# Two transformer layers on one Trainium2 core: longer bank holds in a planned TensorE order, zero products ahead of the first block, nine-step roots, moments by piece

## The chip, the cores and the metric

The kernel runs on one core of a Trainium2 chip. Its engines are TensorE (PE; its weight loads are PEld), VectorE (DVE), ScalarE (ACT), GpSimd (POOL) and SyncE (SP, which here only issues DMAs). The metric is the device time of one execution in microseconds; the median of three runs is given, and one further execution was profiled.

## The reference

4096 tokens (4 sequences of 1024) of width 256 go through two layers, each an attention-like part and a feed-forward part, with a layer norm after each residual sum:

```python
x = L0_attn_x
x = _layernorm(x + _L0_attn_ref(x, W_xproj, dt_bias, A_log, D))     # state-space (SSD), 2 heads, state 64
x = _layernorm(x + _L0_ffn_ref(x, w1, b1, w2, b2))                  # gelu, hidden 1024
x = _layernorm(x + _L1_attn_ref(x, Wqkv, bqkv, Wout, bout, omega, quad_nodes, quad_weights))
x = _layernorm(x + _L1_ffn_ref(x, router_w, expert_bias, w1, w3, w2, sw1, sw3, sw2))
```

`_L0_attn_ref` projects x to a step size and two state vectors, forms decays from their cumulated sums and adds a within-sequence and a carried part. `_L1_attn_ref` is linear attention with 16 heads of width 16: q and k are normalised (a root), projected by omega, and passed through exp (clipped to 20); running sums of k times v and of k are kept, and the result goes through Wout. `_L1_ffn_ref` has two shared experts and eight routed ones of hidden size 512, two per token, all in float32.

## The kernel before, in words

The tokens are cut into 8 blocks of 512, each a tile x0 to x7 of 128 partitions x 4 x 256. Nearly all matrix products are float32; the trace shows a product of 512 columns as two passes.

*Start.* Lines L121 to L138 issue the loads on SP, in the order wx, xt of block 0, vec0, the other even blocks' xt and x, w1, w2, and so on. The first products (`ssd_block`, `project`, L288) need wx_sb and xt of block 0.

*First part, planned.* The work of the first layer, of the second layer's attention and of most of the shared experts is written as small tasks: `ssd_block` for block i; `ffn_block` (turn_x, hidden, outputs); `attn_front` for each half-block hb (turn_x turns the tokens into xTa, project makes q and k, values makes v, turn_qk turns q and k into qkT, features makes qf and kf); `attn_back` (scores, turn_keys, outputs, advance, turn_state, turn, turn_back, project); `attn_tail` (turn_x into xTr, logits, router); then jobs of the shared experts. TensorE executes them in the order in which `trace_tasks` (L248) emits them; the other engines follow a scheduler.

A Task has a cost, a rank, predecessors with a wait for each, and, if it writes PSUM, a pool, a number of banks and a hold. PSUM has 6 banks in pool 0 (SSD, attention, some shared work) and 2 in pool 1 (feed-forward, other shared work). The planner keeps for each pool the times at which its banks come free in its own reckoning, takes at each step the task that can start first (then the lowest rank), and books the task's banks until its end plus hold:

```python
for k in range(task.banks):
    start = max(start, free[task.pool][k] - task.cost * k / task.banks)
...
task.end = now = start + task.cost
for _ in range(task.banks):
    free[task.pool].pop(0)
    free[task.pool].append(now + task.hold)
```

The hold is a plan, no wait: on the chip a bank's next product waits, by semaphore, until the bank has really been copied out. The default hold is 1.5 (L243). The tasks that the change touches are at L466 (turn_x of ffn_block), L583 to L588 (turn_x, project and turn_qk of attn_front), L728 (turn_keys), L737 (turn_back) and L769 (turn_x of attn_tail).

*Dispatch and routed stage.* When the last router product (ps_r) is done, `dispatch` counts on VectorE and GpSimd which token goes to which expert slot, `invert` turns that into lists by products (ps_id), and meanwhile the shared jobs of six blocks run. Then 69 slots of 128 tokens are gathered, put through their expert and added to acc by indirect DMA (`slot_tiles`), in PSUM banks opened anew.

*Tail.* The shared experts of the last two blocks come in pieces (eight of hidden work and four of output, one per tile, for each block; the loop counts them as n, and the block's last four are outputs), between which the eight last layer norms are placed (`last_norm`, L1071), with PE, DVE and ACT in the written order. `sums` takes moments (BATCH_NORM_STATS2 and its aggregate, L1082 and L1083), `scales` the root, `finish` the scaling on ScalarE and the output DMA. For the last block, the first three tiles are normalised after piece 22, the fourth after the last piece.

`rsqrt` (L183) is called by every layer norm and by the q and k normalisation: a guess by an integer shift, then three Newton rounds of three VectorE instructions (L190 to L192).

Of the kernel before, what the change touches and what calls it, by code (L numbers as in the profile page):

```python
# [23 lines left out]
F32 = mybir.dt.float32  # L24
# [52 lines left out]
def two_layers(ctx: ExitStack, tc: tile.TileContext, x, xT, vecs, cols, wx, w1, w2, wqkv, wout, om, rw, moe, out):  # L77
# [19 lines left out]
    def bank(name, n):  # L97

        return psum[n].tile([P, 512], F32, tag="bank", name=name)
# [20 lines left out]
    rw_sb = const.tile([P, KC, VW], F32, name="rw_sb")  # L120
    nc.sync.dma_start(out=wx_sb, in_=wx)  # L121
    nc.sync.dma_start(out=xts[0], in_=xT[0])
    nc.sync.dma_start(out=vec0, in_=vecs[:NVEC0].partition_broadcast(P))
# [59 lines left out]
    def rsqrt(v, shape, tag):  # L183

        r = sm.tile(shape, F32, tag=f"{tag}_r", name=f"{tag}_r")
        s = sm.tile(shape, F32, tag=f"{tag}_s", name=f"{tag}_s")
        nc.vector.tensor_single_scalar(s.bitcast(I32), v.bitcast(I32), 1, ALU.logical_shift_right)  # L187
        nc.vector.tensor_scalar(r.bitcast(I32), s.bitcast(I32), -1.0, float(0x5F3759DF), ALU.mult, ALU.add)  # L188
        for _ in range(3):
            nc.vector.scalar_tensor_tensor(s, r, -0.5, r, ALU.mult, ALU.mult)  # L190
            nc.vector.tensor_mul(s, s, v)  # L191
            nc.vector.scalar_tensor_tensor(r, s, 1.5, r, ALU.add, ALU.mult)  # L192
        return r
# [235 lines left out]
    def ffn_block(i, before, wk):  # L429
# [35 lines left out]
        r = 10.0 + i  # L465
        last = Task(turn_x, 0.9, r, [(ssd_end[i], 10.0), (before, 0.0)], 1, 2)  # L466
        wait = 4.0
# [19 lines left out]
    def attn_front(hb, wk):  # L487
# [94 lines left out]
        used = used_end.get(hb - 2)  # L582
        t_x = Task(turn_x, 0.45, r, [(qk_end.get(hb - 2), 0.0), (ffn_end[i], 10.0), (constants, 0.0), (attention, 0.0)], 0, 1)  # L583
        t_q = Task(lambda: project(0), 1.8, r, [(t_x, 3.5)], 0, 1)
        t_q = Task(lambda: project(1), 1.8, r, [(t_q, 0.0)], 0, 1)
        t_v = Task(values, 1.8, r + 0.1, [(t_x, 3.0), (used, 0.0)], 0, 1)
        t_k = Task(lambda: turn_qk(1), 0.45, r + 0.2, [(t_q, 12.0), (feat_end.get(hb - 1), 0.0)], 0, 1)
        t_q = qk_end[hb] = Task(lambda: turn_qk(0), 0.45, r + 0.2, [(t_k, 0.0)], 0, 1)  # L588
        t_k = Task(lambda: features(1), 0.95, r + 0.3, [(t_k, 5.0), (used, 0.0)], 0, 4, 4.5)
        feat_end[hb] = Task(lambda: features(0), 0.95, r + 0.3, [(t_q, 5.0), (t_k, 0.0), (t_v, 0.0)], 0, 4, 4.5)  # L590

    def attn_back(hb, wk):
# [128 lines left out]
        for j in range(NJ):  # L721
            n = NJ * hb + j
            r = 5.07 + 0.1 * hb + 0.04 * j
            before = at_tile.get(n - 1, {})
            far = at_tile.get(n - 2, {})
            last = hb % 4 == 3 and j == NJ - 1
            t_c = Task(lambda j=j: scores(j), 1.8, r, [(feat_end[hb], 7.0), (before.get("o"), 0.0)], 0, 4, 2.5)
            t_k = Task(lambda j=j: turn_keys(j), 0.9, r + 0.01, [(feat_end[hb], 6.0), (before.get("s"), 0.0)], 0, 2, 2.0)  # L728
            t_o = Task(
                lambda j=j: outputs(j), 1.6, r + 0.02, [(t_c, 3.0), (before.get("kv"), 1.0), (far.get("to"), 0.0)], 0, 2, 1.4  # L730
            )
            at_tile[n] = dict(o=t_o)
            if not last:
                t_s = at_tile[n]["s"] = Task(lambda j=j: advance(j), 0.5, r + 0.03, [(t_k, 2.5), (before.get("kv"), 0.0)], 0, 1)
                at_tile[n]["kv"] = Task(lambda j=j: turn_state(j), 0.25, r - 0.1, [(t_s, 2.0), (t_o, 0.0)], 0, 1)
            t_t = at_tile[n]["to"] = Task(lambda j=j: turn(j), 0.45, r + 0.04, [(t_o, 1.5), (far.get("oT"), 0.0)], 0, 1, 2.5)
            t_t = at_tile[n]["oT"] = Task(lambda j=j: turn_back(j), 0.25, r, [(t_t, 2.0), (far.get("w"), 0.0)], 0, 1)  # L737
            t_w = at_tile[n]["w"] = Task(lambda j=j: project(j), 0.9, r, [(t_t, 2.5)], 0, 1)
        used_end[hb], proj_end[hb] = t_o, t_w

    def attn_tail(i, wk):
# [26 lines left out]
        r = 5.3 + 0.2 * i  # L768
        t_x = turn_end[i] = Task(turn_x, 0.9, r, [(proj_end[2 * i + 1], 10.0), (tail_end.get(i - 1), 0.0)], 0, 2)  # L769
        t_x = Task(logits, 0.5, r, [(t_x, 5.0)], 0, 1)  # L770
# [299 lines left out]

    def last_norm(i, tiles):  # L1071

# [4 lines left out]
        r = None  # L1077

        def sums():
            st = sm.tile([P, NT, 6], F32, tag="ln_st", name=f"ln_st{i}_{tiles[0]}")  # L1080
            for k, j in enumerate(tiles):
                nc.vector.bn_stats(st[:, k, :], xs[i][:, j, :])  # L1082
                nc.vector.bn_aggr(mv[:, k, :], st[:, k, :])  # L1083

# [6 lines left out]
        def finish():  # L1091
# [7 lines left out]
            )  # L1099

        return sums, scales, finish


# [40 lines left out]
    early, amid, late = [0, 1, 2], [3, 4, 5], [6, 7]  # L1144
    with tc.manual_schedule(engines={mybir.EngineType.PE}):
        for i in range(NBLK):
            ssd_block(i, wk0)
# [97 lines left out]
    with tc.manual_schedule(  # L1245
# [8 lines left out]
        for _, kind, *_, piece in jobs:  # L1254
# [9 lines left out]
            if n in norm:  # L1264
                parts.extend(last_norm(*norm[n]))
                if len(parts) == 3:
                    parts.pop(0)()
            if n == 22:
                ends = last_norm(NBLK - 1, whole[:-1])
                ends[0]()  # L1270
                ends[1]()
# [74 lines left out]
```

## Time and profile before

| | |
|---|---|
| three runs | 1566.04, 1570.9 and 1563.34 us; median 1566.04 |
| profiled execution | 1570.37 us, of which its span is 1568.6 us |
| mean granted TensorE clock over the span | 0.983 |
| DVE, ACT, POOL busy | 761.8, 599.2, 420.3 us |
| moved by DMA | 73.55 MB, mean 47 GB/s; busy share near full in the first slice only |
| largest TensorE groups | routed hidden (L1013) 248.5, shared hidden (L941) 225.9, routed output (L1035) 130.7, feed-forward hidden (L441) 123.5 us |

The profile is a record of one execution. A row of a group names line, engine, operation and tiles (written <- read), count, busy time and the mean of one in ns, and the idle time of the engine ahead of it with what ended it. A row of waits reads: who waited <- for whom: us in total, times, longest. A row of a window has its limits and length, then the busy time (and count) of PE, PEld, DVE, ACT and POOL, the granted TensorE clock, the DMA share and GB/s. A row of the timeline has start and length in us, engine and line. Buffer numbers are left out of names: qkT stands for the qkT of every half-block. What the profile calls the granted clock is the share of its full rate that TensorE was given; before the first record it is shown as 1.00.

### The profile page before, as it was taken

Reading aid. Unit: us, or ns where it says so; the run is one execution under the profiler, and the core shown is the slowest. Engines: PE = TensorE matmul, PEld = TensorE weight load, DVE = VectorE, ACT = ScalarE, POOL = GpSimd, SP = SyncE. Lnnn points to the kernel's source line nnn. Section 1 sums busy time; section 2 is a strip of 40 time slices with the busy share of each in tenths; the row PEclk is TensorE's granted clock in tenths of the full one; section 3 lists DMA queues with packets and bytes.
Section 4 is the critical chain, followed back from the end, with each engine's and each line's share of the span. In section 5 each row is a group of like instructions: output and inputs, shape, how many; then the busy total and the mean of one; then the engine's idle time right before and its main releaser. Section 6 shows DMA issues by size and latency. Waiting matters only on the chain. (4 is left out here: it accounts for less than half of the span.)

```text
span 1568.6 us, 25398 instructions
## 1 busy us (share of the span) xinstructions
PE 1493.9 (95%) x9700; PEld 970.0 (62%) x9700; DVE 761.8 (49%) x2411; ACT 599.2 (38%) x1056; POOL 420.3 (27%) x456
## 2 busy tenths in 40 slices
PE   8999989999999989989999999999999999999997
PEld 5566647575857665755765765556666666666554
DVE  5977735665656475575455456122222222222264
ACT  3463373436364625446547411111222222222132
POOL 5623302322122121221110004012444444443100
PEclk9999999999999999999999999999999999999999
DMA  9000000000000000030101043041223223232431
GB/s 328 1 1 1 1 1 2 27 2 1 28 1 15 15 1 28 2 122 1 48 8 55 15 166 136 24 151 41 46 47 46 46 45 47 45 47 35 91 104 54
DMA packets 49654, 73.55 MB, mean 47 GB/s; under 512 B 8416, under 2 KB 42208, under 8 KB 48000
## 3 DMA queue, kind: packets, MB, share of 16 engines
q1 hardware_dynamic: 35856, 52.19, 9.4%
q0 software_dynamic: 13248, 18.17, 7.5%
q8 instruction: 80, 1.31, 0.4%
q10 hardware_dynamic: 432, 1.57, 0.3%
q14 instruction: 38, 0.31, 0.1%
HBM read 45.93 MB, written 25.99 MB: 46 GB/s over the span
## 5 line engine op out<-in xcount | busy, mean ns | idle before, releaser
L1013 PE MATMUL ps_ge<-w,xeT 128*128 x552 | 248.5, 593 | 1.0 <-issue 1.0
L941 PE MATMUL ps_g<-xTs,w 128*128 128x512 f32 x512 | 225.9, 594 | 5.4 <-ACT sl L949 2.6
L941 PEld LDWEIGHTS ps_g<-xTs,w 128*128 128x128 f32 x512 | 95.6, 190 | 119.3 <-issue 106.1
L1013 PEld LDWEIGHTS ps_ge<-w,xeT 128*128 128x128 f32 x552 | 99.5, 190 | 100.6 <-issue 100.6
L1044 POOL DMA_INDIRECT acc<-ye,back x69 | 109.4, 1585 | 110.1 <-DVE xew L1000 75.6
L1023 DVE TENSOR_TENSOR ge<-se,ps_ge 128x512 f32<-128x512 f32 x69 | 47.5, 688 | 178.7 <-PE ps_ge L1013 175.8
L441 PE MATMUL ps_h<-xT,w_sb 128*128 128x512 f32 x256 | 123.5, 627 | 9.1 <-ACT hT L444 5.4
L1035 PE MATMUL ps_ye<-w2e,geT 128*128 x552 | 130.7, 380 | 0.9 <-DVE geT L1030 0.9
L988 POOL DMA_INDIRECT xe<-xt,sent x69 | 68.2, 989 | 228.7 <-PE ps_xe L996 166.3
L453 PE MATMUL ps_f<-w_sb,hT 128*128 128x256 f32 x512 | 117.5, 384 | 0.0
L959 PE MATMUL ps_e<-w,gT 128*128 128x256 f32 x512 | 114.6, 380 | 2.1 <-DVE x L968 2.1
L621 POOL TENSOR_TENSOR sc<-sc,mask_le 128x512 f32<-128x512 f32 x32 | 40.9, 1278 | 275.3 <-ACT sc L620 275.3
L959 PEld LDWEIGHTS ps_e<-w,gT 128*128 128x128 f32 x512 | 96.1, 190 | 18.9 <-DVE x L968 3.7
L1035 PEld LDWEIGHTS ps_ye<-w2e,geT 128*128 128x128 f32 x552 | 99.6, 190 | 12.2 <-ACT ye L1043 1.1
L453 PEld LDWEIGHTS ps_f<-w_sb,hT 128*128 128x128 f32 x512 | 96.8, 192 | 15.9 <-issue 3.4
L950 DVE TENSOR_TENSOR gT<-sl,ps_g 128x512 f32<-128x512 f32 x64 | 43.9, 686 | 115.0 <-PE ps_g L941 92.4
L949 ACT ACTIVATE sl<-ps_g 128x512 f32<-128x512 f32 x64 | 38.0, 596 | 156.7 <-PE ps_g L941 143.4
L441 PEld LDWEIGHTS ps_h<-xT,w_sb 128*128 128x128 f32 x256 | 49.7, 201 | 65.5 <-issue 54.8
L1021 ACT ACTIVATE se<-ps_ge 128x512 f32<-128x512 f32 x69 | 41.3, 599 | 121.5 <-PE ps_ge L1013 121.5
L623 DVE TENSOR_TENSOR sc<-ps_sc,mask_le 128x512 f32<-128x512 f32 x96 | 62.7, 685 | 37.5 <-PE ps_sc L611 30.4
L611 PE MATMUL ps_sc<-qf,kf 64*128 64x128 f32 x1024 | 68.0, 281 | 0.6 <-ACT kf L577 0.5
L1000 DVE TENSOR_TENSOR xew<-xe,nth 128x1 f32<-128x1 f32 x69 | 11.0, 160 | 118.2 <-ACT ye L1043 109.9
(257 smaller groups left out, 2485.5 us busy)
## 6 DMA issues: line engine op xcount, KB each, us to landing
w<-in_moe SPq DMA_DIRECT2D x8, 1024.0 KB, 9.1
xt<-in_xT SPq DMA_DIRECT2D x8, 512.0 KB, 9.6
x<-in_x SPq DMA_DIRECT2D x8, 512.0 KB, 10.8
xt<-x SPq DMA_DIRECT2D x8, 512.0 KB, 3.7
td<-xTr SPq DMA_DIRECT2D x16, 256.0 KB, 2.5
w2e<-in_moe SPq DMA_DIRECT2D x8, 512.0 KB, 7.6
x<-acc SPq DMA_DIRECT2D x8, 512.0 KB, 8.4
out<-x SPq DMA_DIRECT2D x7, 512.0 KB, 2.9
```

The source lines that it names most:

```text
L441: nc.tensor.matmul(ps, w1_sb[:, k, m * P : (m + 1) * P], v.xT[:, k, :], start=(k == 0), stop=(k == KC - 1))
L453: nc.tensor.matmul(v.ps[:, j % 2, :], v.hT[:, m, j * P : (j + 1) * P], w2_sb[:, m, :], start=(m == 0), stop=(m == HID0 // P - 1),)
L611: nc.tensor.matmul(ps[s][:, r * P : (r + 1) * P], kf[rows, r, q, tok], qf[rows, r, q, tok], start=True, stop=True)
L623: nc.vector.tensor_mul(t_s, ps_s, mask)
L941: nc.tensor.matmul(ps[s], w[e][:, 2 * s + k, m * P : (m + 1) * P], xT[i][:, k, :], start=(k == 0), stop=(k == KC - 1),)
L950: nc.vector.tensor_mul(gT[i, e][:, m, :], sl, ps[1])
L959: nc.tensor.matmul(ps, gT[i, e][:, m, j * P : (j + 1) * P], w2e[:, m, :], start=(e == 0 and m == 0), stop=(e == NSH - 1 and m == HID // P ...
L988: nc.gpsimd.indirect_dma_start(out=xe, out_offset=None, in_=xt, in_offset=bass.IndirectOffsetOnAxis(ap=sent[:, s : s + 1], axis=0),)
L1013: nc.tensor.matmul(pg[a], xeT[s][:, k, :], w13[:, bass.ds(e * (4 * HID) + (2 * a + k) * HID, HID)], start=(k == 0), stop=(k == KC - 1),)
L1023: nc.vector.tensor_mul(ge[s], se, pg[1])
L1035: nc.tensor.matmul(ps[:, :D], geT[s][:, m, :], w2[:, bass.ds(of[s] * (2 * HID) + m * D, D)], start=(m == 0), stop=(m == HID // P - 1),)
L1044: nc.gpsimd.indirect_dma_start(out=acc, out_offset=bass.IndirectOffsetOnAxis(ap=back[:, s : s + 1], axis=0), in_=ye, in_offset=None, compu ...
```

## The change

Seven edits. (1) The first loads are split: wx and the first xt each in two halves, one half of wx issued by ScalarE. (2) A tile `idle` is filled with zeros by VectorE, and two products of it with itself, written to a bank that nobody reads, stand ahead of the first real products on TensorE. (3) `rsqrt` has nine instructions instead of eleven: the shift and its correction, a round of third order in four, a Newton round in three, with constants folded. (4) For the last block's first three tiles the moments are taken after pieces 20, 21 and 22, one tile each, instead of all three after piece 22. (5) The tasks turn_x (ffn_block, attn_front, attn_tail) hold their banks 4.0, 3.5 and 4.5 instead of 1.5. (6) project and turn_qk of attn_front hold 2.5 and 4.5 instead of 1.5. (7) turn_keys holds 3.0 instead of 2.0 and turn_back 2.5 instead of 1.5. Holds alter only the planner's reckoning, and so the order in which tasks are emitted; the products themselves stay as they are.

```diff
--- before.py
+++ after.py
@@ -118,8 +118,9 @@
     vec = const.tile([P, NVEC - NVEC0], F32, name="vec")
     col = const.tile([P, NCOL], F32, name="col")
     rw_sb = const.tile([P, KC, VW], F32, name="rw_sb")
-    nc.sync.dma_start(out=wx_sb, in_=wx)
-    nc.sync.dma_start(out=xts[0], in_=xT[0])
+    for n in range(2):
+        (nc.scalar, nc.sync)[n].dma_start(out=wx_sb[:, :, n, :], in_=wx[:, :, n, :])
+        nc.sync.dma_start(out=xts[0][:, n, :], in_=xT[0][:, n, :])
     nc.sync.dma_start(out=vec0, in_=vecs[:NVEC0].partition_broadcast(P))
     for i in range(2, NBLK, 2):
         nc.sync.dma_start(out=xts[i], in_=xT[i])
@@ -182,14 +183,18 @@
 
     def rsqrt(v, shape, tag):
 
+
         r = sm.tile(shape, F32, tag=f"{tag}_r", name=f"{tag}_r")
         s = sm.tile(shape, F32, tag=f"{tag}_s", name=f"{tag}_s")
         nc.vector.tensor_single_scalar(s.bitcast(I32), v.bitcast(I32), 1, ALU.logical_shift_right)
         nc.vector.tensor_scalar(r.bitcast(I32), s.bitcast(I32), -1.0, float(0x5F3759DF), ALU.mult, ALU.add)
-        for _ in range(3):
-            nc.vector.scalar_tensor_tensor(s, r, -0.5, r, ALU.mult, ALU.mult)
-            nc.vector.tensor_mul(s, s, v)
-            nc.vector.scalar_tensor_tensor(r, s, 1.5, r, ALU.add, ALU.mult)
+        nc.vector.tensor_mul(s, r, r)
+        nc.vector.tensor_mul(s, s, v)
+        nc.vector.scalar_tensor_tensor(s, s, -10.0 / 3.0, s, ALU.add, ALU.mult)
+        nc.vector.scalar_tensor_tensor(r, s, 5.0, r, ALU.add, ALU.mult)
+        nc.vector.scalar_tensor_tensor(s, r, -0.5 * 0.375**3, r, ALU.mult, ALU.mult)
+        nc.vector.tensor_mul(s, s, v)
+        nc.vector.scalar_tensor_tensor(r, s, 1.5 * 0.375, r, ALU.add, ALU.mult)
         return r
 
     def transposed(t, i, tiles, n, engines):
@@ -463,7 +468,7 @@
                 layernorm(i)
 
         r = 10.0 + i
-        last = Task(turn_x, 0.9, r, [(ssd_end[i], 10.0), (before, 0.0)], 1, 2)
+        last = Task(turn_x, 0.9, r, [(ssd_end[i], 10.0), (before, 0.0)], 1, 2, 4.0)
         wait = 4.0
         for n in range(4):
             last = Task(lambda n=n: hidden(range(2 * n, 2 * n + 2)), 3.5, r + 0.1 * n, [(last, wait)], 1, 2, 2.2)
@@ -580,12 +585,12 @@
 
         r = 5.0 + 0.1 * hb
         used = used_end.get(hb - 2)
-        t_x = Task(turn_x, 0.45, r, [(qk_end.get(hb - 2), 0.0), (ffn_end[i], 10.0), (constants, 0.0), (attention, 0.0)], 0, 1)
-        t_q = Task(lambda: project(0), 1.8, r, [(t_x, 3.5)], 0, 1)
-        t_q = Task(lambda: project(1), 1.8, r, [(t_q, 0.0)], 0, 1)
+        t_x = Task(turn_x, 0.45, r, [(qk_end.get(hb - 2), 0.0), (ffn_end[i], 10.0), (constants, 0.0), (attention, 0.0)], 0, 1, 3.5)
+        t_q = Task(lambda: project(0), 1.8, r, [(t_x, 3.5)], 0, 1, 2.5)
+        t_q = Task(lambda: project(1), 1.8, r, [(t_q, 0.0)], 0, 1, 2.5)
         t_v = Task(values, 1.8, r + 0.1, [(t_x, 3.0), (used, 0.0)], 0, 1)
-        t_k = Task(lambda: turn_qk(1), 0.45, r + 0.2, [(t_q, 12.0), (feat_end.get(hb - 1), 0.0)], 0, 1)
-        t_q = qk_end[hb] = Task(lambda: turn_qk(0), 0.45, r + 0.2, [(t_k, 0.0)], 0, 1)
+        t_k = Task(lambda: turn_qk(1), 0.45, r + 0.2, [(t_q, 12.0), (feat_end.get(hb - 1), 0.0)], 0, 1, 4.5)
+        t_q = qk_end[hb] = Task(lambda: turn_qk(0), 0.45, r + 0.2, [(t_k, 0.0)], 0, 1, 4.5)
         t_k = Task(lambda: features(1), 0.95, r + 0.3, [(t_k, 5.0), (used, 0.0)], 0, 4, 4.5)
         feat_end[hb] = Task(lambda: features(0), 0.95, r + 0.3, [(t_q, 5.0), (t_k, 0.0), (t_v, 0.0)], 0, 4, 4.5)
 
@@ -725,7 +730,7 @@
             far = at_tile.get(n - 2, {})
             last = hb % 4 == 3 and j == NJ - 1
             t_c = Task(lambda j=j: scores(j), 1.8, r, [(feat_end[hb], 7.0), (before.get("o"), 0.0)], 0, 4, 2.5)
-            t_k = Task(lambda j=j: turn_keys(j), 0.9, r + 0.01, [(feat_end[hb], 6.0), (before.get("s"), 0.0)], 0, 2, 2.0)
+            t_k = Task(lambda j=j: turn_keys(j), 0.9, r + 0.01, [(feat_end[hb], 6.0), (before.get("s"), 0.0)], 0, 2, 3.0)
             t_o = Task(
                 lambda j=j: outputs(j), 1.6, r + 0.02, [(t_c, 3.0), (before.get("kv"), 1.0), (far.get("to"), 0.0)], 0, 2, 1.4
             )
@@ -734,7 +739,7 @@
                 t_s = at_tile[n]["s"] = Task(lambda j=j: advance(j), 0.5, r + 0.03, [(t_k, 2.5), (before.get("kv"), 0.0)], 0, 1)
                 at_tile[n]["kv"] = Task(lambda j=j: turn_state(j), 0.25, r - 0.1, [(t_s, 2.0), (t_o, 0.0)], 0, 1)
             t_t = at_tile[n]["to"] = Task(lambda j=j: turn(j), 0.45, r + 0.04, [(t_o, 1.5), (far.get("oT"), 0.0)], 0, 1, 2.5)
-            t_t = at_tile[n]["oT"] = Task(lambda j=j: turn_back(j), 0.25, r, [(t_t, 2.0), (far.get("w"), 0.0)], 0, 1)
+            t_t = at_tile[n]["oT"] = Task(lambda j=j: turn_back(j), 0.25, r, [(t_t, 2.0), (far.get("w"), 0.0)], 0, 1, 2.5)
             t_w = at_tile[n]["w"] = Task(lambda j=j: project(j), 0.9, r, [(t_t, 2.5)], 0, 1)
         used_end[hb], proj_end[hb] = t_o, t_w
 
@@ -766,7 +771,7 @@
             nc.scalar.copy(v.lT, ps)
 
         r = 5.3 + 0.2 * i
-        t_x = turn_end[i] = Task(turn_x, 0.9, r, [(proj_end[2 * i + 1], 10.0), (tail_end.get(i - 1), 0.0)], 0, 2)
+        t_x = turn_end[i] = Task(turn_x, 0.9, r, [(proj_end[2 * i + 1], 10.0), (tail_end.get(i - 1), 0.0)], 0, 2, 4.5)
         t_x = Task(logits, 0.5, r, [(t_x, 5.0)], 0, 1)
         tail_end[i] = Task(lambda: router(i, v.lT), 0.15, r, [(t_x, 3.5)], 0, 1)
 
@@ -1068,7 +1073,7 @@
             turn_tokens(NFULL, wx)
             run(range(NFULL, NSLOT), lambda: None)
 
-    def last_norm(i, tiles):
+    def last_norm(i, tiles, split=False):
 
 
         n = len(tiles)
@@ -1076,11 +1081,15 @@
         mv = sm.tile([P, NT, 2], F32, tag="ln_mv", name=f"ln_mv{i}_{tiles[0]}")
         r = None
 
+        st = sm.tile([P, NT, 6], F32, tag="ln_st", name=f"ln_st{i}_{tiles[0]}")
+
         def sums():
-            st = sm.tile([P, NT, 6], F32, tag="ln_st", name=f"ln_st{i}_{tiles[0]}")
             for k, j in enumerate(tiles):
-                nc.vector.bn_stats(st[:, k, :], xs[i][:, j, :])
-                nc.vector.bn_aggr(mv[:, k, :], st[:, k, :])
+                moments(k, j)
+
+        def moments(k, j):
+            nc.vector.bn_stats(st[:, k, :], xs[i][:, j, :])
+            nc.vector.bn_aggr(mv[:, k, :], st[:, k, :])
 
         def scales():
             nonlocal r
@@ -1098,6 +1107,8 @@
                 out=out.rearrange("b (n c p) d -> (b n) p c d", c=NT, p=P)[i, :, at, :], in_=xs[i][:, at, :]
             )
 
+        if split:
+            return moments, scales, finish
         return sums, scales, finish
 
 
@@ -1143,6 +1154,12 @@
     nc.sync.dma_start(out=acc[NTOK:, :], in_=spare_rows)
     early, amid, late = [0, 1, 2], [3, 4, 5], [6, 7]
     with tc.manual_schedule(engines={mybir.EngineType.PE}):
+
+        idle = wkf.tile([P, TB], F32, name="idle")
+        nc.vector.memset(idle, 0.0)
+        ps = bank("ps_idle", 0)
+        for _ in range(2):
+            nc.tensor.matmul(ps, idle[:, :P], idle, start=True, stop=True)
         for i in range(NBLK):
             ssd_block(i, wk0)
         before = None
@@ -1265,9 +1282,11 @@
                 parts.extend(last_norm(*norm[n]))
                 if len(parts) == 3:
                     parts.pop(0)()
+            if n == 20:
+                ends = last_norm(NBLK - 1, whole[:-1], True)
+            if 20 <= n < 23:
+                ends[0](n - 20, n - 20)
             if n == 22:
-                ends = last_norm(NBLK - 1, whole[:-1])
-                ends[0]()
                 ends[1]()
         ends[2]()
         for part in last_norm(NBLK - 1, whole[-1:]):
```

## The prediction

> **What bounds the kernel now.** I read the page's busy times first, then the windows, TensorE's waits, the start and the end.
>
> ```profile
> PE 1493.9 (95%) x9700; PEld 970.0 (62%) x9700; DVE 761.8 (49%) x2411; ACT 599.2 (38%) x1056; POOL 420.3 (27%) x456
> ```
>
> TensorE is the bound: 1568.6 of span less 1493.9 leaves 74.7 us idle. A stage can gain only that idle time, and products that ran at a reduced clock. The windows (length, then busy time of PE, PEld, DVE, ACT, POOL; then granted clock) show where both lie:
>
> ```profile
> 0.00:200.00 200.00, 187.30 (x932) 123.12 (x932) 149.25 (x667) 90.05 (x158) 88.15 (x171) 0.98 0.19 65
> 200.00:900.00 700.00, 651.77 (x6387) 449.20 (x6388) 393.39 (x1129) 360.52 (x606) 136.97 (x135) 0.97 0.06 21
> 900.00:1475.00 575.00, 570.91 (x2126) 349.42 (x2124) 170.24 (x412) 122.89 (x245) 193.60 (x149) 1.00 0.29 64
> ...
> 447.79:451.20 3.41, 2.89 (x10) 2.38 (x11) 0.00 (x0) 3.38 (x5) 0.53 (x1) 0.50 0.00 0
> ```
>
> 48.2 us of idle lie between 200 and 900 us, where attention is interleaved with feed-forward blocks; the routed stage after 900 us has 4. In the last row TensorE worked at clock 0.50. Going through the windows I find twelve such pieces of 3.41 us between 200 and 900 us, with 38 us of TensorE work in them, so half of that, 19 us, is lost to the clock. Each stands behind idle time: this one behind gaps of 0.93 and 2.53 us at 443.7 and 445.8. 19 us over 48 us of gaps is 0.4 us of clock per us of gap.
>
> Who ends TensorE's waits (total, times, longest):
>
> ```profile
> PE ps_k L633 <- ACT qkT L551: 8.2, 4, 2.5
> PE ps_p L564 <- ACT qkT L551: 7.1, 6, 2.9
> ...
> PE ps_bc L288 <- DMA xt<-in_xT: 5.1, 1, 5.1
> PE ps_oT L708 <- DVE o L701: 4.0, 2, 3.6
> ...
> PE ps_p L564 <- DVE x L717: 3.2, 3, 1.8
> ...
> PE ps_k L633 <- ACT xTa L208: 1.4, 1, 1.4
> ```
>
> The first row tells most. ps_k doesn't read qkT: it waits for the PSUM bank that the copy to qkT has still to empty. The same holds of ps_k behind xTa, ps_p behind x. Walking through all gaps with the program's semaphores, some 30 of the 48 us are such bank waits, 18 are waits for data.
>
> **The change, part by part.**
>
> *Holds.* No instruction is added. The planner frees a bank `hold` us after its task, in its own reckoning, and gives it to the next task. In the trace the copy of ps_qkT ends 0.6 to 11.3 us after the last product, median 4.8; the hold was 1.5 and becomes 4.5. I compared the two built orders: how much TensorE work, at the trace's mean durations, stands between the last product into a bank and the first that reuses it. Behind qkT, 5 of 17 reuses had only 2.05 to 2.2 us before; after, 2 of 19 have under 2.3, the others over 5.3. Behind xTa: 5 of 11 under 2.1, then 2 of 10. The rearrangement reaches banks whose hold is unchanged: behind kf the shortest goes from 1.04 to 2.75, behind qf from 1.04 to 4.69, behind x eight under 2 become two. Against the median delay of each kind of evacuation, shortfalls over 200 to 900 us add up to 47.7 us before (the gaps are 48) and 30.1 after: 17.6 less. That is the high end. The low end is what the lengthened holds directly name, 8.2 + 1.4 = 9.6 us. With 0.4 us of clock for each: 13.4 to 24.6.
>
> Here rule and trace part. The Trainium skill, "TensorE: Matmul & The Clock Gate", section "Why this matters for your kernels", allows idle gaps up to about 3 us before the clock drops. Only three gaps of 200 to 900 us could then matter (2.90, 2.95 and 3.56 us), and removing gaps of 1.3 to 2.5 us would bring no clock: 9.6 to 17.6 us. The trace has half-clock pieces behind gaps of 1.3 us (57.6) and of 0.46 and 1.34 us (202); I take the trace.
>
> Against it stands ScalarE. In the new order its table loads grow from 82 to 90; a load takes 1283 ns, so 10.3 us on the engine that ends 32 of the 48 us of waits. It is 52% busy there (360.5 of 700), so they cost nothing where a copy isn't waiting behind them, and 10.3 us where one always is. I take a fifth, 2 us. Also, at the end of attention ps_oT now twice follows the product behind its o, and ps_w once that behind its oT, with nothing between them: 1.56 + 1.56 + 0.41 us by their medians, counted in the 30.1. For the middle: halfway between 13.4 and 24.6 is 19; less 2, less a margin of 1 for neighbours displaced, gives **16 us**.
>
> *Order of stages.* More shared-expert work is used as filling during attention, so the last router product stands at 790 us of accumulated TensorE work in place of 769, and 117 us of work remain ahead of the first routed product, formerly 138. The dispatch needs 35 us on VectorE and GpSimd (927.5 to 962.5), and after its inversion some 16 us of w2e loads: covered, nothing.
>
> *Head.* First product 5.11 us, when xt has landed. Timeline:
>
> ```profile
> 5.11 6.54 PE L288 MATMUL ps_bc<-xt,wx_sb 128*128 128x512 f32 x8 [5.11 <-DMA xt<-in_xT]
> ...
> 11.92 1.88 PE L288 MATMUL ps_bc<-xt,wx_sb 128*128 128x512 f32 x4
> ```
>
> Eight passes in 6.54 us, 0.82 each; later four in 1.88: 0.47. Passes stay slow until about 10.9, 5.8 us after the start. The added chain: one VectorE fill of 128x512, bounded by a fill of 128x16 (0.10 us) and a GpSimd fill of this size (0.53); from 0.9 it ends by 1.5. Then four slow passes, 3.4 us, to 4.95, so the loads' wait is covered: the first half-loads are 128 and 256 KB and start at 0.8, where the whole loads landed at 3.56 and 4.98. If full speed comes again 5.8 us after the first pass, at 7.3, real work at time t is (7.3-4.95)/2 + t-7.3 = t-6.1, formerly (10.9-5.1)/2 + t-10.9 = t-8.0: **1.9 us** gained. The same page, section "What you observe", puts the change about 4 us into activity; then it would be 5.5 and 2.8 us. I keep the row. Bounds: 0.2 us lost, if the fill or the loads are late (zero passes queue ahead of the real ones), to 2.8 gained. Splitting wx puts one issue ahead of ScalarE's first table load (about 0.5 us); ScalarE's first wanted result comes at 8.9, so nothing. On SP every later load is issued one issue (0.47 us) later: xt of the second block landed at 8.97, and its product, at 11.92 before, would now come at about 9.9; half a microsecond of cover is left, and without it up to 0.5 is lost.
>
> *Tail.* The chain that ended last, in order of time:
>
> ```profile
> 1549.67 7.19 PE ps_e L959 x32
> ...
> 1561.32 0.16 DVE ln_v L1089
> 1561.48 0.34 DVE x L968
> ...
> 1564.85 0.17 DVE ln_v L1089
> 1565.04 0.60 ACT x L1093
> ```
>
> The last product ends at 1561.1, but x's add starts at 1561.40, because three tiles' moments and their root still occupy VectorE. Two of three pairs (0.53 us a pair) move ahead of it: they run while TensorE is in the next tile's 3.4 us of products, and the add queued behind them waits for those anyway. And the root loses two steps (0.2 us each): 1.4 us freed, of which 0.3 are used. The last tile's own root saves 0.39. **0.7 us**, nearly certain.
>
> *Roots elsewhere.* 49 roots lose two steps, 98 instructions of 0.16 to 0.24 us on an engine busy 49%: covered by products. Where a data wait runs through them (qk to qkT, xT behind a layernorm) they could give up to 1.5 us; I count zero.
>
> **Sum.** 16 + 1.9 + 0.7 = 18.6. Profiled execution 1570.4 us (span 1568.6 and 1.8 around it): 1551.8. It lay 4.3 above the median of the three runs, 1566.0; from that median, **1547.5**.
>
> **Rivals.**
> A, forecast: bank waits go, clock pieces go with them: 1547.5, from 1537 to 1558. Chance 0.71.
> B, the middle gains nothing: waits move from banks to data (the 18 us of waits for qkT, o, oT, xTr have unchanged distances in the planner). Only head and tail stay: 1566.0-2.6 = 1563.4. For it: ps_p behind qkT keeps 3.87 to 4.3 us of work against a median delay of 4.8. Against it: the bank distances in the built order are longer. Chance 0.20.
> C, slower: ScalarE decides. The eight more table loads stand ahead of evacuations that TensorE waits for, each returns 1.28 us and its clock share, and no bank wait is saved: 10.3 x 1.4 = 14.4, 1566.0-2.6+14.4 = 1577.8. It decides once the loads lie in front of more waits than the holds remove, that is once exposed loads exceed 9.6 us. Against it: ScalarE idles 48% of that time. Chance 0.09.
>
> Faster by over 0.5% (below 1558.2; 0.5% is about what a measurement here can tell from no change): 0.71. Within it: 0.20. Slower: 0.09. The range leaves out C and the best of A: 1537 to 1566.
>
> **What would show it.** Right: idle from 200 to 900 us near 36 instead of 48; half-clock pieces there eight or nine instead of twelve; ps_k behind qkT under 3 us; passes fast by 7 to 8 us; the last add directly behind the last product. Wrong: qkT's copy later than 4.8 us in the median behind more table loads (C), or waits for qkT, o, oT as data grown by what the bank waits lost (B).

## The result and the profile after

The changed kernel takes 1589.3 us (median of four runs, 1585.88 to 1590.7), the kernel before beside it 1567.07 (1563.34 to 1570.9): ratio 1.0138, 95% interval 1.0108 to 1.0169. It is 22 us slower. The profiled execution took 1590.7 us, its span 1588.8, at a mean clock of 0.981.

The page's busy row of the changed kernel:

```profile
PE 1501.6 (95%) x9704; PEld 970.0 (61%) x9704; DVE 746.9 (47%) x2314; ACT 609.3 (38%) x1064; POOL 418.8 (26%) x456
```

TensorE is idle 87.2 us of the span (1588.8 less 1501.6), formerly 74.7, and its busy time grew by 7.7 us, of which 3.8 are the zero products. The windows of the changed kernel, with the routed stage's limits moved to where it now begins:

```profile
0.00:200.00 200.00, 189.27 (x940) 124.26 (x940) 148.15 (x647) 91.10 (x160) 87.81 (x171) 0.98 0.19 65
200.00:900.00 700.00, 643.16 (x6010) 435.27 (x6011) 367.47 (x1023) 346.56 (x578) 134.45 (x133) 0.97 0.06 21
900.00:1495.00 595.00, 585.00 (x2500) 362.31 (x2498) 184.99 (x458) 144.99 (x278) 194.96 (x151) 0.99 0.28 62
```

From 200 to 900 us the idle time is 56.8 us: it rose by 8.6 where it should have fallen by 12. The third window now holds 10.0 us of idle. The first routed product (ps_ge) starts at 1091.3 us, formerly 1070.3, and from there to the end it is 497.5 us against 498.3: the whole loss lies ahead of the routed stage. There the gaps over 0.15 us after the first 20 us add up to 72.6 us (56.5 before), and the half-clock pieces (3.41 us each at a granted clock of 0.50, 17 of them for 14 before) hold 51.0 us of TensorE work (44.7), half of it lost: 16.1 + 3.2 = 19.3 of the 21.0.

TensorE's waits in the changed kernel (in total, times, longest):

```profile
PE ps_h L446 <- ACT hT L449: 12.8, 11, 2.0
PE ps_p L569 <- ACT qkT L556: 9.3, 5, 2.9
PE ps_g L946 <- ACT sl L954: 8.3, 7, 1.8
PE ps_oT L713 <- DVE o L706: 7.1, 4, 3.5
PE ps_w L720 <- ACT oT L715: 5.8, 3, 3.7
```

Three of these rows in the kernel before, which the prediction did not show:

```profile
PE ps_h L441 <- ACT hT L444: 5.4, 4, 2.1
PE ps_w L715 <- ACT oT L710: 2.9, 1, 2.9
PE ps_g L941 <- ACT sl L949: 2.6, 3, 1.4
```

The rows that the holds name are gone: no ps_k behind qkT (8.2 before), none behind xTa (1.4), and the wait of ps_p for x is 1.5 (3.2). What the five rows of the changed kernel gained is more: hT +7.4 and sl +5.7, waits for banks of the feed-forward and shared-expert work that serves as filling (other products put into the gaps); qkT +2.2, o +3.1 and oT +2.9, data that attention waits for. At the end of attention the timeline of the changed kernel shows the last two:

```profile
933.71 0.66 PE L700 MATMUL ps_to<-ident,oraw 128*128 128x128 f32 x4
936.08 0.41 PE L713 MATMUL ps_oT<-ident,o 128*128 128x128 f32 x2 [1.71 <-DVE o L706]
...
937.75 1.08 PE L655 MATMUL ps_o<-sc,v 128*32 128x128 f32 x16
938.76 2.08 PE L720 MATMUL ps_w<-wout_sb,oT 128*128 128x256 f32 x4
940.63 0.88 PE L700 MATMUL ps_to<-ident,oraw 128*128 128x128 f32 x4
942.81 0.41 PE L713 MATMUL ps_oT<-ident,o 128*128 128x128 f32 x2 [1.30 <-DVE o L706]
943.69 1.21 PE L720 MATMUL ps_w<-wout_sb,oT 128*128 128x256 f32 x4 [0.46 <-ACT oT L715]
```

ps_oT stands directly behind the product whose result it reads through VectorE; nothing fills the 1.3 to 1.7 us. Together the three waits shown are 3.5 us, what the prediction put them at; the other 9.4 us for o and oT lie earlier. The ps_w at 938.76 takes 2.08 us where the one at 943.69 takes 1.21, for the same four products: the windows of the same kernel, cut where the clock changes, say why.

```profile
934.37:937.78 3.41, 1.70 (x54) 0.97 (x55) 1.49 (x5) 0.37 (x1) 0.52 (x1) 1.00 0.00 0
937.78:941.19 3.41, 3.41 (x29) 2.53 (x24) 0.32 (x1) 0.74 (x2) 0.00 (x0) 0.50 0.02 5
941.19:944.61 3.42, 1.65 (x9) 1.13 (x8) 1.23 (x6) 0.37 (x1) 0.00 (x0) 1.00 0.00 0
944.61:948.02 3.41, 3.41 (x9) 2.71 (x9) 2.67 (x13) 0.00 (x0) 0.00 (x0) 0.50 0.00 0
```

The two ps_w lie in different clocks. A stretch with 1.70 or 1.65 us of TensorE work in 3.41 is followed by one at clock 0.50 (last section).

Head and tail gave what was forecast, the head not in the way forecast (below). Timeline of the changed kernel's start, and the chain that ended last:

```profile
1.53 3.78 PE L1162 MATMUL ps_idle<-idle 128*128 128x512 f32 x4 [1.53 <-DVE run L852]
5.10 4.02 PE L293 MATMUL ps_bc<-xt,wx_sb 128*128 128x512 f32 x8
...
10.15 1.96 PE L293 MATMUL ps_bc<-xt,wx_sb 128*128 128x512 f32 x4
```

```profile
1578.36 3.73 PE ps_e L964 x16
1582.12 0.43 DVE x L973
...
1585.18 0.17 DVE ln_v L1098
1585.38 0.60 ACT x L1102
```

The eight passes take 4.02 us instead of 6.54, the next four start 1.77 us earlier, and x's add stands directly behind the last product.

### The profile page after: what moved, and what is told of

It is laid out like the page before. It is cut to its first block, busy times and chain, and to the rows that moved or that the text cites. A ratio compares the mean times of both kernels' runs of the same rounds, so it can differ in the third digit from the quotient of the medians.

```text
span 1588.8 us, 25316 instructions
## 1 busy us (share of the span) xinstructions
PE 1501.6 (95%) x9704; PEld 970.0 (61%) x9704; DVE 746.9 (47%) x2314; ACT 609.3 (38%) x1064; POOL 418.8 (26%) x456
## 5 line engine op out<-in xcount | busy, mean ns | idle before, releaser
L1048 ACT ACTIVATE ye<-ps_ye,xew 128x256 f32<-128x256 f32 x69 | 32.6, 473 | 92.6 <-PE ps_ye L1040 92.6
```

## The experiments

Times are medians in us; ratios are to the kernel before on the same chip (its medians 1568.1 to 1568.9), with 95% intervals. The expectations name five theories. Bank theory is the prediction's: a longer hold pays where it names a wait. S: table loads of ScalarE stand ahead of evacuations (the copies that empty a PSUM bank). P: the holds only moved the waits to the two banks of pool 1. O: each new order of TensorE is a draw, whatever the planner was told. D, formed after the first eight runs: a longer distance between two uses of a bank (the TensorE work in between) is paid with a shorter distance in attention's data chain, where turn_back reads o and project reads oT.

**Without the holds** (all longer holds back to their old values; roots, head and tail changed):

```diff
-            t_k = Task(lambda j=j: turn_keys(j), 0.9, r + 0.01, [(feat_end[hb], 6.0), (before.get("s"), 0.0)], 0, 2, 3.0)
+            t_k = Task(lambda j=j: turn_keys(j), 0.9, r + 0.01, [(feat_end[hb], 6.0), (before.get("s"), 0.0)], 0, 2, 2.0)
...
-        t_x = turn_end[i] = Task(turn_x, 0.9, r, [(proj_end[2 * i + 1], 10.0), (tail_end.get(i - 1), 0.0)], 0, 2, 4.5)
+        t_x = turn_end[i] = Task(turn_x, 0.9, r, [(proj_end[2 * i + 1], 10.0), (tail_end.get(i - 1), 0.0)], 0, 2)
```

> The changed kernel with all seven hold arguments put back; zero products, split loads, nine-step roots and moments by piece stay. Theory S (the loss comes from the new order: ScalarE loads tables 90 times instead of 82 and empties ps_h and ps_g later): head and tail alone, 1567.1 - 1.7 - 0.9 = 1564.5 us, idle from 200 to 900 us about 48, waits of ps_h for hT about 5.4. Rival (another part costs, the roots or the zero products moving VectorE's schedule): over 1580.

1571.06; 1.0022 (1.0011 to 1.0033). So the holds cost some 18 of the 22 us, and what is left, head, tail and roots, does not give the 2.6 us of gain that was forecast for head and tail either.

**Holds one by one.** The first keeps only turn_qk's 4.5, the second only turn_keys' 3.0, the third all but turn_qk's. Against the kernel without holds, the first and then the second:

```diff
-        t_q = qk_end[hb] = Task(lambda: turn_qk(0), 0.45, r + 0.2, [(t_k, 0.0)], 0, 1)
+        t_q = qk_end[hb] = Task(lambda: turn_qk(0), 0.45, r + 0.2, [(t_k, 0.0)], 0, 1, 4.5)
...
-            t_k = Task(lambda j=j: turn_keys(j), 0.9, r + 0.01, [(feat_end[hb], 6.0), (before.get("s"), 0.0)], 0, 2, 2.0)
+            t_k = Task(lambda j=j: turn_keys(j), 0.9, r + 0.01, [(feat_end[hb], 6.0), (before.get("s"), 0.0)], 0, 2, 3.0)
```

> Of the holds only that of turn_qk (4.5). Its built order has 92 table loads. Theory S: as slow as the whole change or nearly, 1582 to 1592, with ps_k behind qkT gone and waits for hT and sl grown. Rival, bank theory of the prediction (the hold pays where it names a wait): 8.2 us and their clock less, 1553 to 1558. Rival O (any new order is a draw, table loads have nothing to do with it): anywhere, no relation to the loads.

> Of the holds only that of turn_keys (3.0 for 2.0). Its order has 92 table loads; before, no gap stood behind a kt bank. Theory S: 1578 to 1592. Bank theory: nothing to gain, 1564. Rival O: anywhere.

> The change without the hold of turn_qk. Its order has 84 table loads. Theory S: near the kernel without holds, 1564 to 1572, ps_k behind qkT back at some 8 us. Bank theory: 8.2 us and their clock worse than the whole change, over 1597. Rival O: anywhere.

1580.62 (1.0082, 1.0063 to 1.0101), 1579.49 (1.0067, 1.0049 to 1.0085), 1584.74 (1.0101, 1.0081 to 1.0122), with 92, 92 and 84 table loads against 82. No single hold is the culprit, and the number of loads doesn't order the times: the slowest of the three has the fewest, 84 (the whole change has 90 and takes 1589.3). The third lies in neither of the ranges written down for S and for the bank theory. In the first, ps_k behind qkT is gone as named, but ps_p behind qkT rose to 11.2 and hT to 8.4.

**No table loads between gelu, silu and exp**: gelu and silu are replaced by relu in the kernel before and in the changed one (5 loads each). The values change; the instructions themselves take as long (hT 691 ns with relu for 686, sl 596 in both).

```diff
-                nc.scalar.activation(v.hT[:, m, :], ps, AF.Gelu, bias=col[:, m : m + 1])
+                nc.scalar.activation(v.hT[:, m, :], ps, AF.Relu, bias=col[:, m : m + 1])
...
```

> The kernel before with gelu and silu replaced by relu (a changed computation), which needs no table of its own: 5 table loads in place of 82, the order on TensorE as before. It is the base of the next run. With 77 loads of 1.28 us gone from ScalarE, waits for hT, sl and qkT should fall in any theory: 1535 to 1555 us.

> The changed kernel with the same replacement: 5 table loads, the new order on TensorE as it is. Theory S (table loads make the new order slow): the 18 to 22 us between the two orders shrink to under 6, both near 1545. Theory P (the order itself: attention's banks counted busy for longer let feed-forward and shared products stand closer behind each other than pool 1's two banks and ScalarE can follow, table loads or not): at least 12 us remain.

1540.57 (0.9813, 0.9799 to 0.9827) and 1553.08 (0.9895, 0.9881 to 0.9909). The distance in time between the two kernels falls from 22 to 12.5 us: the loads, or where they now lie, carry some 10 us. That is less than S expected (under 6 us left), and barely what P set as its least (12). TensorE's waits in the changed kernel with relu:

```profile
PE ps_oT L713 <- DVE o L706: 7.1, 4, 3.5
PE ps_p L569 <- ACT qkT L556: 7.1, 5, 2.4
PE ps_w L720 <- ACT oT L715: 6.3, 3, 4.1
```

The bank wait for hT is down to 0.5 us and that for sl gone; o and oT stand as high as with gelu. In the kernel before with relu they have 4.0 and 3.3.

**Holds for the filling work too** (feed-forward hidden 2.2 to 4.5, shared jobs 2.0 to 4.0, on top of the change):

```diff
-            last = Task(lambda n=n: hidden(range(2 * n, 2 * n + 2)), 3.5, r + 0.1 * n, [(last, wait)], 1, 2, 2.2)
+            last = Task(lambda n=n: hidden(range(2 * n, 2 * n + 2)), 3.5, r + 0.1 * n, [(last, wait)], 1, 2, 4.5)
...
-            jobs.append(Task(job, cost, 100.0, after, n, banks, 2.0))
+            jobs.append(Task(job, cost, 100.0, after, n, banks, 4.0))
```

> The changed kernel with the holds of the filling work lengthened too: hidden of ffn_block 4.5 for 2.2 and the shared jobs 4.0 for 2.0, about what the trace shows for the copies to hT (median 4.5). 84 table loads. Theory P (waits were moved from pool 0 to the two banks of pool 1): ps_h and ps_g behind hT and sl fall from 21 to under 10 us and the time to 1560 to 1575. Theory S, by the loads: 1568 to 1573. Theory O (the planner's reckoning has no hold on the real waits, any new order is a draw): 1575 to 1590 like the others.

1620.0; 1.0319 (1.0304 to 1.0334). TensorE's waits there:

```profile
PE ps_w L720 <- ACT oT L715: 11.9, 6, 4.1
PE ps_oT L713 <- DVE o L706: 9.7, 4, 6.2
PE ps_sc L616 <- DVE qf L584: 6.6, 3, 4.0
PE ps_txTr L211 <- ACT sc L625: 5.3, 1, 5.3
PE ps_g L946 <- ACT sl L954: 4.7, 4, 2.0
PE ps_h L446 <- ACT hT L449: 4.7, 3, 2.1
```

The banks of pool 1 got their distance (21.1 to 9.4 us), and the time rose by 31 us. Waits came back elsewhere: o and oT together 21.6 us (12.9 in the changed kernel), qf 6.6, a bank that the copy to sc empties 5.3. The half-clock pieces ahead of the routed stage rose from 17 to 26. P names a place of the waits, not the cause of the loss. The median of 4.5 us for copies to hT, from which the 4.5 was taken, is too high for all of them (3.2 us from 200 to 900 in the changed kernel); the section on the prediction says why one median fits badly.

**Roots alone, head and tail alone.** The first has only the nine-step rsqrt; the second only zero products, split loads and moments by piece. Both keep TensorE's old order. In rsqrt the first has the added lines, the second the removed ones (the rest as in the kernel before and the changed kernel):

```diff
-        for _ in range(3):
-            nc.vector.scalar_tensor_tensor(s, r, -0.5, r, ALU.mult, ALU.mult)
...
+        nc.vector.tensor_mul(s, r, r)
+        nc.vector.tensor_mul(s, s, v)
...
```

> The kernel before with the nine-step roots alone; the order on TensorE is that of before, those of VectorE and ScalarE may shift. The kernel without holds was 3 us slower than head and tail allow. If the roots shift the other engines' orders to TensorE's cost: 1570 to 1573 (0.1 to 0.3% slower). If not (the head or chance): 1566.5 to 1569, as before or 0.5 us faster.

> The change without its holds and with the old eleven-instruction roots: only the zero products, the split first loads and the moments by piece remain, and TensorE's order is that of before. If head and tail pay what the changed kernel's profile shows (bc2 at 10.15 in place of 11.92 us, the last 0.8 us): 2.5 us under the kernel before, ratio 0.9984, and the first routed product near 1068.6 instead of 1070.3. If shifting the whole schedule by 1.7 us disturbs the orders on ScalarE and VectorE as the shorter roots did: 0 to 3 us slower.

1572.84 (1.0025, 1.0013 to 1.0037) and 1569.83 (1.0015, 1.0004 to 1.0025). Neither gains. With the roots TensorE is idle 55.7 us ahead of the routed stage, no more than before, but has 16 half-clock pieces in place of 14. With head and tail it runs ahead, by 1.8 us near 540 us, and loses that lead there at one place (last section).

**The chain cut** (turn_back and project read a constant; order and banks stay), in the changed kernel and in the one before:

```diff
-                nc.tensor.transpose(ps[:, c * P : (c + 1) * P], o[j][:, c * P : (c + 1) * P], ident)
+                nc.tensor.transpose(ps[:, c * P : (c + 1) * P], ident, ident)
...
-                nc.tensor.matmul(ps[:, :D], oT[j][:, c, :], wout_sb[:, c, :], start=(c == 0), stop=(c == KC - 1))
+                nc.tensor.matmul(ps[:, :D], ident, wout_sb[:, c, :], start=(c == 0), stop=(c == KC - 1))
```

> The changed kernel with one chain cut: turn_back and project read a constant in place of o and oT (what attention computes never reaches x), every instruction, its place in TensorE's order and the bank waits stay. Theory D (holds lengthen the bank distance and shorten the distance in attention's chain o, oT, w, where TensorE then waits for data): ps_oT<-o and ps_w<-oT (12.9 us, and 0.4 us of clock for each) go, 14 to 18 us faster than the changed kernel, about 1572 to 1575. Theory S (ScalarE's table loads ahead of evacuations): the waits move to the next evacuation and only 3 to 6 us go, 1584 to 1587.

> The kernel before with the same cut. It has 6.9 us of these waits, so 7 to 10 us faster than the kernel before, about 1558 to 1560. What counts is the distance between the two cut kernels: theory D expects the 22 us between the kernels to fall to 12 to 15; if this chain is only where the loss happens to be seen, the distance stays near 22.

1573.63 (1.0034, 1.0023 to 1.0045) and 1565.04 (0.9977, 0.9967 to 0.9987). The cut gives the changed kernel 15.7 us, as D expected, and the kernel before 3.9, less than the 7 to 10 expected: the distance between the two falls from 22 to 8.6, further than D's 12 to 15. TensorE's first waits in the changed kernel with the cut:

```profile
PE ps_h L446 <- ACT hT L449: 16.0, 11, 2.0
PE ps_p L569 <- ACT qkT L556: 9.3, 5, 2.9
PE ps_g L946 <- ACT sl L954: 8.3, 7, 1.8
```

The other waits stay, hT 3.2 us higher. Ahead of the routed stage the gaps fall by 7.4 us and the half-clock pieces from 17 to 8 (51.0 us of work to 25.8), so in this execution more comes back through the clock, 12.6 us, than through the gaps. D's direction is borne out; two of its three sizes are not.

**Longer data waits in the plan**, with the holds and without them (here with the old roots):

```diff
-            t_t = at_tile[n]["oT"] = Task(lambda j=j: turn_back(j), 0.25, r, [(t_t, 2.0), (far.get("w"), 0.0)], 0, 1, 2.5)
-            t_w = at_tile[n]["w"] = Task(lambda j=j: project(j), 0.9, r, [(t_t, 2.5)], 0, 1)
+            t_t = at_tile[n]["oT"] = Task(lambda j=j: turn_back(j), 0.25, r, [(t_t, 4.0), (far.get("w"), 0.0)], 0, 1, 2.5)
+            t_w = at_tile[n]["w"] = Task(lambda j=j: project(j), 0.9, r, [(t_t, 4.5)], 0, 1)
```

> The changed kernel with the planner's data waits lengthened as well, o to turn_back from 2.0 to 4.0 and oT to project from 2.5 to 4.5. Theory D: the planner puts other products between, ps_oT<-o and ps_w<-oT (12.9 us) fall under 5, and the time to 1572 to 1580. Theory O (every new order is a draw, whatever the planner was told): anywhere from 1575 to 1600, with these waits replaced by others.

> Head, tail and old roots, no holds, but the planner's data waits lengthened: o to turn_back from 2.0 to 4.0, oT to project from 2.5 to 4.5. The fourth cell beside neither (1569.8), holds only (1589.3), holds and waits (1573.6). Theory D (the two distances compete for the same filling work; the holds alone took it from the data waits): ps_oT<-o and ps_w<-oT (6.8 us in the kernel before) fall under 3, the time to 1562 to 1567, as the cut of this chain gave 1565.0. Theory O (each new order is a draw that costs some us): 1571 to 1585; 90 table loads in place of 82 would then be part of it.

1573.57 (1.0035, 1.0025 to 1.0045) and 1573.27 (1.0035, 1.0021 to 1.0048). The first is the time that D expected, 16 us back, but of its two waits only that for o went (7.1 to 0.2). The one for oT stayed, so the two together are 6.8 us where D expected under 5:

```profile
PE ps_w L720 <- ACT oT L715: 6.6, 3, 3.9
```

The second is a miss of D, in the range written down for O: no gain on the kernel before. Its waits:

```profile
PE ps_h L442 <- ACT hT L445: 11.3, 8, 2.1
PE ps_kv L689 <- DVE den L699: 9.1, 2, 5.2
PE ps_p L565 <- ACT qkT L552: 5.6, 5, 2.2
```

o is gone from its rows and oT down to 0.7 as planned, and 9.1 us of a wait that the kernel before doesn't have (ps_kv behind den) and 5.9 more for hT came in. So with these waits holds and new roots together cost nothing, and without them 19.5 us (1589.3 against 1569.8); the roots alone measured 4.0.

**More data waits** (qkT to features 5.0 to 7.5, xTr to logits 5.0 to 6.5, on top of the last), without and with the holds:

```diff
-        t_k = Task(lambda: features(1), 0.95, r + 0.3, [(t_k, 5.0), (used, 0.0)], 0, 4, 4.5)
+        t_k = Task(lambda: features(1), 0.95, r + 0.3, [(t_k, 7.5), (used, 0.0)], 0, 4, 4.5)
...
-        t_x = Task(logits, 0.5, r, [(t_x, 5.0)], 0, 1)
+        t_x = Task(logits, 0.5, r, [(t_x, 6.5)], 0, 1)
```

> As the kernel with longer waits alone, and also qkT to features from 5.0 to 7.5 and xTr to logits from 5.0 to 6.5 in the plan. 78 table loads. Theory D: ps_p<-qkT (7.0 us) and ps_l<-xTr (3.0) go too, bank waits behind qkT (8.2) stay: 1550 to 1562. Theory O: 1570 to 1585.

> The changed kernel with all the longer data waits: holds, o to turn_back 4.0, oT to project 4.5, qkT to features 7.5, xTr to logits 6.5. 82 table loads. If holds and waits add up (each distance can be had at once): bank and data waits both fall, 1545 to 1558. If the filling work is too little for both: the gaps come back as waits for hT and sl, the banks of the filling work itself, 1568 to 1585.

1577.2 (1.0056, 1.0037 to 1.0075) and 1593.61 (1.0171, 1.0155 to 1.0188). The first misses D's range (1550 to 1562) and lies in O's. In the second, holds and roots cost 16 us again, with o at 0.2 and oT at 2.2 but hT at 16.6 and sl at 11.0. D alone therefore does not tell in which order holds cost. The other case written down, too little filling for both distances, has the place right (waits for hT and sl), but the time is above its range of 1568 to 1585.

**Both suspects taken away** (relu and the cut together):

> The changed kernel with relu for gelu and silu, and with o and oT cut from attention's chain as before. What counts is its distance to the kernel before with the same two edits. Theory D and S as two separate causes (12.5 us of distance left without table loads, 8.6 without the chain, of 22): 12.5 + 8.6 - 22 = about -1, so -4 to 3 us. One cause seen twice, or a third one: 7 to 9 us left. In itself 1535 to 1545.

> The kernel before with relu and the cut chain: its relu version ran 1540.6 and has 7.3 us of waits for o and oT there; the cut gave 3.9 us with gelu and silu. 1533 to 1538.

1536.24 (0.9807, 0.9789 to 0.9826) and 1533.19 (0.9779, 0.9763 to 0.9795). Of 22 us of distance 3.0 are left, at the edge of what two separate causes allow (-4 to 3): 9.7 by the loads and 13.6 by the chain are 23.3 taken one at a time, 19.2 taken together, so some 4 us belong to both. No version built here that still computes the reference beats the kernel before.

## Why the prediction was wrong, step by step

*The step that failed* is the count of the holds: "Against the median delay of each kind of evacuation, shortfalls over 200 to 900 us add up to 47.7 us before (the gaps are 48) and 30.1 after: 17.6 less." The count came within 0.5 us of the old order's gaps, from which its delays were taken. In the new order the gaps of that stretch are 56.8, not 30.1. The distances were read off the built order, so by elimination it is the delays that failed, and the traces bear it out: a delay is no property of an evacuation. Of the 64 copies to hT, 27 have a table load directly ahead of them on ScalarE, in both orders; from the last product to the end of the copy they take 4.1 us in the median before and 5.6 after, the other 37 take 0.7 in both. Over all copies to hT from 200 to 900 us the median went from 1.7 to 3.2. One median for such a kind fits neither half, and the planner books nothing of what stands ahead on ScalarE.

*The low end was no bound.* 9.6 us, the rows that the holds name, did go in full. But in the same order the five other rows rose by 21. The bank distances were longer by the prediction's own count, which is what it held against rival B, and still the time rose.

*Data distances.* The prediction saw it ("ps_oT now twice follows the product behind its o, and ps_w once that behind its oT, with nothing between them") and put it at 3.5 us by medians, inside the 30.1. Those three waits are 3.5 us in the trace (1.71 + 1.30 + 0.46), so their size was right. What was missed is their clock (two pieces at 0.50 stand behind them) and 2.5 us more of such waits elsewhere: in all 12.9 us against 6.9, and cutting them is worth 15.7 us against 3.9.

*ScalarE.* "I take a fifth, 2 us" for the eight extra loads was too low, if all that the new places of the loads cost is counted: without any loads the distance between the kernels shrinks by 9.7 us. Yet rival C, which counts loads, names the wrong quantity: 84 loads ran slower than 92. Where the loads lie fits better: as many stand ahead of copies to hT as before, but these copies end later. The sign written down for C, qkT's copy later than 4.8 us in the median, did not come: 4.2 us from 200 to 900, against 4.6 before. C's mechanism carries some 10 of the 22 us; its "no bank wait is saved" is wrong, since the named ones were saved. Rival B ("waits move from banks to data") carries some 14, with 4 in common, and was mis-sized: it let the waits move at no cost, and they grew.

*Clock.* 0.4 us for each us of gap was a fair average of the order before. Siding with the trace was right: pieces at half clock stand behind a gap of 1.7 us, and behind gaps of 1.3 and 0.5, where the Trainium skill ("TensorE: Matmul & The Clock Gate", section "Why this matters for your kernels") allows gaps of about 3 us. From 200 to 900 us there are 13 such pieces where eight or nine were forecast and 12 stood before.

*Head*: 1.77 us for 1.9 forecast, in part by luck. The clock rose at 5.93 us, not at 7.3; by itself that gives half of the 1.4 us more. But with the loads split, vec landed at 8.87 us (7.73 before), ScalarE's first copy to bc started only at 8.98, and ps_dtb waited 0.57 us for it, where the prediction counted nothing for ScalarE. With head and tail alone the clock rose at 7.24 us, nearly as forecast, and the four passes came 1.88 us earlier. *Tail*: 0.8 for 0.7, right in place and size. Together they are worth nothing in the median (1569.83 against 1568.88); in the profiled execution the lead of the head is lost on the way. *Roots elsewhere*: forecast nothing to 1.5 us of gain, alone they measured 4.0 us of loss by medians. *Order of stages*: covered, as forecast; ahead of the first routed product TensorE waits 0.83 us in both kernels, and nothing was lost behind it.

What stays open: why just these orders put their waits where they do. The cut and relu settle in which waits the loss lies, not a rule by which the planner could avoid it. D failed as such a rule: the waits without holds and more waits without holds both missed its range, and with the holds more waits didn't help. O is not refuted: all nine new orders that were run, the change included, came out slower than the kernel before, by 5 to 51 us, and this may be what any departure from that order costs. Nor was a wait cut that both kernels share, to see how far any relief brings two kernels together.

## What to carry to other kernels

Evacuation delays read from a profile hold for the order they were read in, and a median hides that some copies stand behind a table load and others don't. When a planner changes the order of one engine, look at the queues of the engines that evacuate, and don't call a wait that goes away a lower bound for the gain. A planned distance between producer and reader is, as the runs here suggest, bought with filling work: count how much filling there is before lengthening one kind of distance, and look for the other kind that shortens. Cutting a suspected wait in the changed kernel and in the one before, and comparing the distance between the two, measures what that wait carries, its clock included. The rows of waits alone mislead: a wait that is lost in one place returns in another.

## What the runs showed of the hardware

The half-clock pieces lie on a grid of time, not behind a certain gap. In each of the 19 profiles all of them start a whole number of 3.413 us apart (58.67 and 144.00 in the kernel before are 25 of them apart), with another offset from the start in each. Adding up TensorE's busy time in each 3.41 us stretch of that grid, 23 of the 27 drops of the clock in the two kernels' profiles follow a stretch with at most 51% of work, and only four stretches so empty were not followed by a drop. After a half-clock stretch of at least 82% the clock is back; after the six of 44 to 80% it stayed at half. So the same gap costs a piece or nothing, by where it falls. The wait of ps_k for qkT near 540 us is 2.53 us long both in the kernel before and in the one with head and tail alone. The windows of the kernel before on its grid:

```profile
536.63:540.04 3.41, 2.17 (x25) 1.50 (x23) 1.61 (x4) 3.38 (x6) 1.27 (x1) 1.00 0.00 0
540.04:543.45 3.41, 1.92 (x13) 1.81 (x14) 0.69 (x1) 3.38 (x6) 0.00 (x0) 1.00 0.02 5
```

and those of the kernel with head and tail alone, where everything runs 1.8 us earlier:

```profile
536.31:539.72 3.41, 0.88 (x17) 0.46 (x13) 2.27 (x3) 3.38 (x6) 0.87 (x1) 1.00 0.00 0
539.72:543.13 3.41, 3.41 (x12) 3.11 (x13) 0.00 (x0) 3.38 (x5) 0.00 (x0) 0.50 0.03 5
```

In the first the gap is split between two stretches, both over half busy, and the clock stays. In the second it lies in one, which is busy 0.88 of 3.41 us, and the next runs at 0.50: by 549 us the lead is 0.2 us. That is where the head's gain went in this execution. Over 143 executions of the kernel before, the time goes with the mean clock (correlation -0.88): 28 with a clock of 0.9875 or more have a mean of 1564.6 us, 64 under 0.9845 have 1569.9. A change of 2 us far from the end can thus be lost in a spread of some 5 us.

The clock's first rise is on the grid too: at 5.93 us in the changed kernel, 4.4 us after its first zero pass; at 10.88 in the kernel before and 7.24 with head and tail alone, 5.8 and 5.7 us after their first passes. Over the 19 profiles it comes 2.9 to 5.8 us after the first pass, so what zero products ahead of the first block gain can differ by over a microsecond from one execution to the next (an estimate: half of that difference).
